# Issuing the sixteen block transfers of each head group from one queue instead of two

## Chip, core and metric

The kernel runs on one NeuronCore of a Trainium2 chip. The metric is the device time of one execution in microseconds (us); several runs are given by their median. The engines are named as the profile names them: PE (TensorE, matrix products), DVE (VectorE), ACT (ScalarE), POOL (GpSimd) and SP (SyncE). SP computes nothing here: it only issues transfers (DMAs). ACT computes and also issues some transfers. "SPq" and "ACTq" in the profile are the issuing of transfers by these two engines.

## What is computed

A decoder layer on `x` of 4 batches of 1024 tokens with 256 features: self-attention, cross-attention to 64 context tokens, and a routed feed-forward part, each on a layer norm of `x` and added to `x`. All is in float32. The part that matters here is the self-attention, with 16 query heads, 4 key/value heads and a head size of 64:

```python
qkv = hidden_states @ qkv_w.T + qkv_b
xq, xk, xv = jnp.split(qkv, [H * D, H * D + KV * D], axis=-1)
...
xq = xq * scale[None, None, None, :]
xk = jnp.repeat(xk, rep, axis=2)
xv = jnp.repeat(xv, rep, axis=2)
scores = jnp.einsum('bqhd,bkhd->bhqk', xq, xk)
probs = jax.nn.softmax(scores.astype(jnp.float32), axis=-1).astype(xq.dtype)
out = jnp.einsum('bhqk,bkhd->bqhd', probs, xv)
out = out.reshape(B, S, H * D)
return out @ o_w.T + o_b
```

## The kernel before

**The unit of work.** A "duo" (function `duo`, line 561 on) is the attention of 4 heads for one tile of 128 query tokens of one batch. There are 4 batches x 8 query tiles x 4 duos = 128 duos. For each of the 4 heads PE computes the scores of 128 queries against 1024 keys (line 587), DVE takes the maximum of each row (line 601), ACT writes the exponentials into the tile `prob` and sums them (line 607), and DVE transposes each 32x32 block in place (line 616). PE needs the weights with the keys on the partitions, so the blocks must also be exchanged between the four groups of 32 partitions. That is done by sixteen transfers from the tile `prob` to the tile `probT`, for each pair of a source group `qb` and a target group `r` (lines 638 to 653, function `carry`). Each moves 32 partitions x 1024 float32, 128 KB, within the on-chip memory. Then PE multiplies the transposed weights by the values (line 668, tile `av`), and ACT copies the result to `heads` (line 683). After four duos `project` (line 688) divides by the sums and applies the output projection; for that three more transfers go through SP (line 714 `rsD`, and line 704 twice, `rb`).

**Who issues the sixteen.** The loop over `k` and `qb` issues them in four rounds of four. Rounds 0, 1 and 2 go through SP's queue (12 transfers), round 3 through ACT's (4 transfers), where they stand among ACT's own instructions. Each engine works its instructions in order, so an instruction that waits holds up all that stand behind it.

**Buffers.** `prob` and `probT` of all duos share four places of 16 KB per partition (`prob=4` in the table of places). A duo takes one for `prob` before its first exponential and one for `probT` before its first transfer. By the planner's allotment the places go round: in 107 of the 127 duos after the first, `probT` takes the place that held `prob` of the duo ahead of it, so that its first transfer must wait until all sixteen transfers of the duo ahead have landed. In most of the others it takes the place of an earlier `probT` and waits for that one's `av`.

**The order of the work.** Nothing is issued directly. Each step is recorded as a task with an engine, an assumed cost in us, the tiles that it reads and writes, and a due time (`flow.add`). The planner (`Flow.order`) then plays the tasks through with these costs and fixes in which order each engine's instructions are issued, and which place each buffer gets. The chip runs these fixed orders and synchronizes by semaphores. The costs given to the sixteen transfers are 0.68 on SP and 0.45 on ACT, and a landing time of 2.3 (`lag`). In the trace the transfers share eight completion semaphores (100 to 105, 107 and 108) that are given out in turn; a transfer waits until the one that had its semaphore before it, eight transfers back, has landed.

Of the kernel before, what the change touches and what calls it, by code (L numbers as in the profile page):

```python
# [77 lines left out]
class Flow:  # L78
# [14 lines left out]
    def add(self, engine, cost, key, emit, reads=(), writes=(), lag=None, holds=(), lead=False, urgent=False):  # L93
        t = Task(engine, cost, emit, key, self.LAG.get(engine, 0.0) if lag is None else lag)
        t.lead, t.urgent = lead, urgent or lead
        for b in reads:
            t.need.update(b.writers)
        for b in writes:
            t.need.update(b.readers)
        t.need.discard(t)  # L100
        for b in reads:
            b.readers.append(t)
        for b in writes:
            b.writers.append(t)
        for b in dict.fromkeys(x.whole for x in (*reads, *writes, *holds)):
            if b.tag is None:
                continue
            if not b.uses:
                t.takes.append(b)
                b.first = t  # L110
                if b.tag not in self.shared:
                    self.lines.setdefault(b.tag, []).append(b)
            elif b.first is not t:
                t.need.add(b.first)
            b.uses.add(t)
            t.bufs.append(b)
        self.tasks.append(t)
        return t
# [71 lines left out]
def decoder(  # L190
# [21 lines left out]
    nc = tc.nc  # L212
# [238 lines left out]
    def by_array(d):  # L451

        return False
# [107 lines left out]
    def duo(b, d):  # L561
# [16 lines left out]
        for i in range(2):  # L578
# [17 lines left out]
            for z in range(2):  # L596
                k = z * QC + c
# [37 lines left out]
        if not by_array(d):  # L635


            for k in range(4):
                for qb in range(4):
                    r = (qb + k) % 4  # L640

                    engine, queue, cost = ("ACT", nc.scalar, 0.45) if k == 3 else ("SP", nc.sync, 0.68)

                    def carry(qb=qb, r=r, queue=queue):
                        queue.dma_start(  # L645
                            out=probT.t[32 * r : 32 * r + 32, S * qb : S * (qb + 1)],
                            in_=prob.t[32 * qb : 32 * qb + 32, S * r : S * (r + 1)],
                        )

                    add(  # L650
                        engine, cost, at, carry, [prob.part((z, i)) for z in range(2) for i in range(2)],
                        [probT.part((z, g)) for z in range(2) for g in range(2)], lag=2.3,
                    )
# [529 lines left out]
    for b in range(B):  # L1183
        at = float(b * steps_of)
        normed(b, lambda g: at - 18 + 2 * g if b else -50 + g)
        for w in range(NT // 2):
            if w == 0:
                keys(b, 0, at - 5)
            for c in range(0, QC, 2):
                queries(b, w, c, at + 2 * QC * w + c - 5)  # L1190
            if w == 0:
                keys(b, 1, at - 1)
                for g in range(NT // 2):
                    value_rows(b, g, at + g / 2)
                for g in range(NT // TF):
                    load_x(b, g, at + 2 + 4 * g * QC)
                context(b, at + 10)
            for d in range(QC * w, QC * w + QC):
                duo(b, d)
                if d % (QC // 2) == QC // 2 - 1:  # L1200
                    project(b, d // (QC // 2))
            t = 2 * w + 1
            cross_attention(b, t - TX + 1, at + QC * (t + 1) + 3)
            last = TX if (b, t // TF) == (B - 1, NT // TF - 1) else TF
            if t % last == last - 1:
                feed_forward(b, t - last + 1, last, at + QC * (t + 1) + 10)
# [93 lines left out]
```

## Time and profile before

| | us |
|---|---|
| median of 3 runs | 1967.02 |
| lowest and highest run | 1962.63 and 1979.3 |
| the profiled execution | 1969.67 |
| its span (first to last instruction) | 1968.0 |
| PE busy in the span | 1664.0 |
| DVE busy | 1535.9 |
| ACT busy | 929.0 |
| POOL busy | 556.0 |
| issues of `probT<-prob` by SP / by ACT | 1536 / 512 |

The profile shows one execution. "Busy" leaves out the issuing of transfers, so ACT's 929.0 us hold nothing of the 512 transfers that it issues. Idle time of an engine is put down to what ended it. The chain of work that ended last follows the execution backwards from its end, at each step to what released it; its shares tell which work the end time hung on. The granted clock of PE is 0.916 of full speed as a mean over the span.

### The profile page before, as it was taken

The page shows a single profiled execution, that of the slowest core. Times are in us where ns is not written, and L with a number is a line of the kernel's source. Part 1 is how long each engine was busy: PE and PEld are TensorE (multiplying, and loading weights), DVE is VectorE, ACT ScalarE, POOL GpSimd, SP SyncE. Part 2 cuts the span into 40 slices and gives each one's busy share as a digit, 9 for nine tenths or more (in the row PEclk, how much of TensorE's full clock was granted, in tenths as well). Part 3 has the DMA queues.
Part 4 walks back from the last instruction along what each step waited for, and adds up shares of the span by engine and source line. Part 5 has one row for each costly group of instructions (what it writes and reads, how often), then busy time and mean ns, then how long its engine had stood idle before and what let it go on. Part 6 is the DMA issues. An engine that isn't in the chain of part 4 may idle for free.

```text
span 1968.0 us, 27927 instructions
## 1 busy us (share of the span) xinstructions
PE 1664.0 (85%) x9156; PEld 936.4 (48%) x9156; DVE 1535.9 (78%) x2164; ACT 929.0 (47%) x1721; POOL 556.0 (28%) x872
## 2 busy tenths in 40 slices
PE   6898997889998798889989788888999888887632
PEld 4454554545555454444545444444555544453321
DVE  4887887888788787798778878887879978789432
ACT  3454554545455454544445445554545545453211
POOL 1001222252222522243031522215112251214352
PEclk8999999989999999889999899988999999898755
DMA  3777777577675777567677577656767577765500
GB/s 132 182 184 189 180 174 185 132 189 184 153 183 125 178 188 177 129 154 181 161 179 175 129 177 188 153 147 167 172 168 183 135 176 178 176 157 129 132 13 12
DMA packets 120032, 310.14 MB, mean 158 GB/s; under 512 B 36560, under 2 KB 47568, under 8 KB 119888
## 3 DMA queue, kind: packets, MB, share of 16 engines
q1 hardware_dynamic: 91504, 229.39, 48.4%
q10 hardware_dynamic: 25680, 69.52, 14.6%
q0 software_dynamic: 2704, 9.46, 1.6%
q8 instruction: 74, 1.21, 0.3%
q14 instruction: 70, 0.57, 0.1%
HBM read 35.32 MB, written 4.46 MB: 20 GB/s over the span
## 4 chain that ended last, share of the span: by engine, by line
PE 40%; DMA 19%; DVE 14%; SPq 12%; ACT 5%; issue 5%; POOL 3%; ACTq 2%; DVEq 0%; POOLq 0%
PE av L668 16%; DMA probT<-prob 16%; PE s L587 12%; SPq L645 11%; DVE nmax L601 6%; PE po L725 3%; ACT prob L607 3%; DVE prob L616 3%; ACTq L645 2%; DMA rb<-rsD 1%; PE pq L540 1%; PE pk L489 1%; PE pxt L895 1%; PE pxp L929 1%; PE pv L512 1%
## 5 line engine op out<-in xcount | busy, mean ns | idle before, releaser
L607 ACT ACTIVATE prob<-s,nmax 128x1024 f32<-128x1024 f32 x512 | 569.2, 1113 | 530.1 <-DVE nmax L601 444.4
L601 DVE TENSOR_REDUCE nmax<-s 128x1 f32<-128x1024 f32 x512 | 599.4, 1211 | 192.8 <-PE s L587 191.2
L616 DVE STREAM_TRANSPOSE prob<-prob 128x1024 f32<-128x1024 f32 x512 | 612.1, 1221 | 69.7 <-ACT prob L607 56.6
L668 PE MATMUL av<-probT,vn 128*64 128x256 f32 x4096 | 543.6, 420 | 110.3 <-DMA probT<-prob 50.8
L587 PE MATMUL s<-kT,qT 64*128 64x512 f32 x2048 | 583.8, 628 | 34.7 <-ACT prob L607 34.7
L668 PEld LDWEIGHTS av<-probT,vn 128*64 128x64 f32 x4096 | 321.1, 151 | 349.6 <-issue 183.4
L587 PEld LDWEIGHTS s<-kT,qT 64*128 64x128 f32 x2048 | 213.0, 190 | 271.1 <-issue 177.2
L707 POOL TENSOR_TENSOR heads<-heads,rb 128x256 f32<-128x256 f32 x128 | 91.4, 734 | 517.6 <-DMA rb<-rsD 353.1
L540 PE MATMUL pq<-ln_T,wq 128*128 128x256 f32 x512 | 127.0, 392 | 1.5 <-ACT heads L683 0.8
L725 PE MATMUL po<-wo,heads 128*128 128x256 f32 x512 | 125.5, 389 | 1.7 <-POOL heads L707 1.4
L683 ACT COPY heads<-av 128x256 f32<-128x256 f32 x128 | 47.2, 369 | 152.8 <-PE av L668 137.3
L725 PEld LDWEIGHTS po<-wo,heads 128*128 128x128 f32 x512 | 92.7, 190 | 40.4 <-issue 17.7
L540 PEld LDWEIGHTS pq<-ln_T,wq 128*128 128x128 f32 x512 | 94.2, 192 | 35.8 <-issue 11.1
L860 POOL TENSOR_TENSOR xsc<-xsc,xmx 128x1024 f32<-128x1024 f32 x32 | 60.9, 1904 | 162.6 <-DVE xmx L857 158.2
L607 ACT ACTIVATION_READ_ACCUMULATOR prob<-s,nmax 128x1 f32 x512 | 100.3, 196 | 0.0
L551 ACT ACTIVATE qT<-pq,bqs,qscale 128x256 f32<-128x256 f32 x128 | 66.7, 564 | 34.2 <-PE pq L540 21.9
L882 POOL TENSOR_TENSOR xsc<-xsc,xrs 128x1024 f32<-128x1024 f32 x32 | 60.8, 1901 | 56.5 <-DVE xrs L879 56.0
L895 PE MATMUL pxt<-ident,xsc 128*128 128x128 f32 x256 | 43.9, 302 | 36.0 <-POOL xsc L882 31.1
L422 ACT ACTIVATE ln_n<-x,ln_mv,ln_rs 128x256 f32<-128x256 f32 x64 | 36.5, 595 | 72.5 <-POOL ln_mv L417 63.9
L414 POOL TENSOR_SCALAR ln_rs<-ln_mv 128x1 f32<-128x1 f32 (+1 forms) x96 | 21.4, 223 | 168.7 <-DVE ln_mv L410 150.2
L1120 POOL DMA_INDIRECT par<-in_table,tile x32 | 32.4, 1012 | 128.8 <-DVE tile L1109 122.9
L436 PE MATMUL ln_pt<-ident,ln_n 128*128 128x128 f32 x192 | 35.3, 306 | 37.1 <-ACT ln_n L422 28.7
(163 smaller groups left out, 1385.5 us busy)
## 6 DMA issues: line engine op xcount, KB each, us to landing
probT<-prob SPq DMA_DIRECT2D x1536, 128.0 KB, 3.1
probT<-prob ACTq DMA_DIRECT2D x512, 128.0 KB, 3.7
rb<-rsD SPq DMA_DIRECT2D x64, 256.0 KB, 4.2
ln_n<-in_x SPq DMA_DIRECT2D x16, 256.0 KB, 3.1
x<-in_x SPq DMA_DIRECT2D x8, 512.0 KB, 4.1
out<-ln_n POOLq DMA_DIRECT2D x7, 512.0 KB, 4.9
wq<-in_w_qT ACTq DMA_DIRECT2D x1, 1024.0 KB, 8.2
wo<-in_w_oT SPq DMA_DIRECT2D x1, 1024.0 KB, 12.7
```

The lines of the kernel that those rows point to most:

```text
L540: mm(pq.t[:, 2 * P * k : 2 * P * (k + 1)], lhsT=wq[:, dc, (c + k) * P : (c + k + 1) * P], rhs=xTs[b].t[:, dc, 2 * P * w : 2 * P * (w + 1)] ...
L551: nc.scalar.activation(qTs[b, w, c + k].t, pq.t[:, 2 * P * k : 2 * P * (k + 1)], AF.Identity, bias=bqs[:, c + k : c + k + 1], scale=qscale,)
L587: mm(ps[z].t[:, 512 * g : 512 * (g + 1)], lhsT=q.t[r, (qt % 2) * P : (qt % 2 + 1) * P], rhs=kT.t[r, 512 * g : 512 * (g + 1)], start=True, ...
L601: nc.vector.tensor_reduce(nmax.t, ps[z].t, AX.X, ALU.max, negate=True)
L607: nc.scalar.activation(weights(prob.t, z, i), src, AF.Exp, bias=nmax.t, accum_out=ss.t[:, k : k + 1])
L616: nc.vector.transpose(t, t)
L645: queue.dma_start(out=probT.t[32 * r : 32 * r + 32, S * qb : S * (qb + 1)], in_=prob.t[32 * qb : 32 * qb + 32, S * r : S * (r + 1)],)
L668: mm(av.t[r, : 2 * P], lhsT=vns[b, kc // 2].t[:, kc % 2, j * HD : (j + 1) * HD], rhs=rhs, start=(kc == 0), stop=(kc == NT - 1),)
L707: nc.gpsimd.tensor_tensor(hT[e].t, hT[e].t, rb.t[:, 2 * e : 2 * e + 2, :], ALU.mult)
L725: mm(po.t[:, :D], lhsT=hT[c // 2].t[:, c % 2], rhs=wo[:, c, :], start=(c == 0), stop=(c == QC - 1))
L860: nc.gpsimd.tensor_tensor(sc.t, sc.t, mx.t.unsqueeze(2).to_broadcast([P, XH, SK]), ALU.subtract)
L895: flip(pt.t[:, j * P : (j + 1) * P], flat[:, c * P : (c + 1) * P], ident)
```

## The change

All sixteen transfers are issued from SP's queue. The assumed cost, which the planner uses, becomes 0.64 for each. The transfers themselves, their order in the loop, their tiles and their sizes stay the same.

```diff
             for k in range(4):
                 for qb in range(4):
                     r = (qb + k) % 4
 
-                    engine, queue, cost = ("ACT", nc.scalar, 0.45) if k == 3 else ("SP", nc.sync, 0.68)
+                    engine, queue, cost = ("SP", nc.sync, 0.64)
 
                     def carry(qb=qb, r=r, queue=queue):
                         queue.dma_start(
```

Since the planner decides all orders, the changed engines and costs also move other instructions. In both versions each query tile's three transfers `rsD` and `rb` stand between or within these groups on SP's queue. On PE, the first `av` product of a duo stands on average 1.89 duos of score products behind its own scores before the change and 1.91 after it; it stands exactly two duos behind in 84 of the 128 duos before and in 109 after, and one and a half behind in 33 before and in 17 after. `probT` takes the place of the `prob` of the duo ahead in 107 of 127 duos before and in 121 after.

## Prediction

> **What bounds the kernel now.** I read the busy times first, then the chain that ended last, then one stretch where it is simple, then SP's queue, and last the waits of PE and ACT.
>
> ```profile
> PE 1664.0 (85%) x9156; PEld 936.4 (48%) x9156; DVE 1535.9 (78%) x2164; ACT 929.0 (47%) x1721; POOL 556.0 (28%) x872
> ...
> PE 40%; DMA 19%; DVE 14%; SPq 12%; ACT 5%; issue 5%; POOL 3%; ACTq 2%; DVEq 0%; POOLq 0%
> ```
>
> PE is the busiest engine, yet only 40% of the chain is PE's. DMA and SPq together have 31%: for a good part of the time the end hangs on issuing and landing transfers. The chain from 60 to 1800 us (start and end left out), and then from 100 to 130 us:
>
> ```profile
> by line: DMA probT<-prob 17.5%; PE av L668 17.3%; PE s L587 12.9%; SPq L645 12.9%; DVE nmax L601 5.9%; issue 4.5%; PE po L725 3.3%; ACT prob L607 3.1%; DVE prob L616 2.4%; ACTq L645 2.0%; DMA rb<-rsD 1.6%; PE pq L540 1.3%; PE pxt L895 1.0%;
> ```
> ```profile
> by line: DMA probT<-prob 49.5%; SPq L645 46.4%; issue 4.1%; ACT prob L607 3.9%; ACTq L645 0.5%
> ```
>
> From 100 to 130 the block transfers alone are 95.9% of the chain, though PE is busy 29.08 of these 30 us: there both bind. SP's timeline shows how. The first row is one duo's burst on SP, the second its last eight transfers alone, the third the start of the next burst; the fourth is ACT's share of the first burst, from ACT's timeline.
>
> ```profile
> 146.31 9.48 SPq L645 DMA_DIRECT2D probT<-prob  x12
> ...
> 150.79 5.00 SPq L645 DMA_DIRECT2D probT<-prob  x8
> ...
> 157.79 0.51 SPq L645 DMA_DIRECT2D probT<-prob  x1
> ```
> ```profile
> 146.21 2.83 ACTq L645 DMA_DIRECT2D probT<-prob  x4
> ```
>
> The burst ends at 155.79 and the next begins 2.00 us later, when the last transfer has landed, because the next `probT` takes the place of this `prob`. So bursts are a serial chain: burst, landing, burst, here with a period of 157.79 - 146.31 = 11.48 us. Over the trace 82 of 127 bursts start so: 1.6 to 3.5 us behind the burst ahead (mean 2.2), over 0.5 us after their own transposes were done. In the burst SP and ACT issue together at first; the eight that SP issues alone come every (5.00 - 0.59) / 7 = 0.63 us, at 0.59 us each by the median in this view, whose last line is the landing:
>
> ```profile
> L645 SPq DMA_DIRECT2D probT<-prob x1536: 507/590/2257, 50.8 to 1850.7; - x192
> L645 ACTq DMA_DIRECT2D probT<-prob x512: 513/613/2090, 53.1 to 1839.2; - x171
> ...
> DMA to landing us min/median/max: 2.2/3.2/6.9
> ```
>
> Last, what SP, then PE and ACT (60 to 1800 us), wait for:
>
> ```profile
> SPq L645 <- DMA probT<-prob: 340.8, 289, 5.3
> ...
> SPq L645 <- PE av L668: 80.1, 15, 14.9
> ```
> ```profile
> PE av L668 <- DMA probT<-prob: 49.4, 23, 3.7
> PE s L587 <- ACT prob L607: 32.9, 26, 2.8
> ```
> ```profile
> ACT prob L607 <- DVE nmax L601: 421.8, 182, 8.5
> ...
> ACT prob L607 <- DMA probT<-prob: 49.9, 14, 6.6
> ```
>
> PE waits at `av` for transfers more than for anything else; ACT mostly waits for DVE, so it has time to spare.
>
> **The change, part by part.** The sum is made against the profiled execution: span 1968.0, with 1.67 us around it 1969.67. It lies 2.65 us above the median 1967.02.
>
> *Four more issues on SP in each burst.* Alone on SP, sixteen take 15 x 0.63 + 0.59 = 10.04 us, against 9.48 in the burst shown: +0.56. The 93 bursts that nothing else interrupts have a median of 9.47 and a mean of 9.73, so +0.57 or +0.31. I take 0.56, since the mean contains late semaphores. Below, a gain is possible: all bursts, with `rsD` and `rb` inside and ACT's part counted, last 10.39 on average, 0.35 more than 10.04. Above, at the mean pitch of today's bursts (10.39 / 12 = 0.87, transfers delaying each other) sixteen would take 13.9: +3.5. I take 0.63, because it is the row of transfers on SP alone.
>
> How many count: SPq and DMA of these transfers are 30.4% of 1740 us = 529 us of the chain. Where nothing else binds they are 95.9% of it, so this is worth 529 / 0.959 = 552 us of pure burst chain, or 552 / 11.48 = 48 periods. 48 x 0.56 = **+27 us**. Bounds: 23 duos in which PE visibly waits at `av` for a landing, x 0.31 = +7; all 82 chained bursts x 0.56 = +46.
>
> *The landing behind a burst* stays 2.0: it comes after issues that SP already makes alone today. The wait for the semaphore of eight transfers back goes: on one queue that one was issued 8 x 0.63 = 5.04 us earlier, and landings have a median of 3.2. Today's burst contains such a wait (149.84 to 150.79); its going is within the 10.04.
>
> *Four issues taken from ACT.* All 512 take 340 us of ACT's queue (mean 0.66), and waiting for semaphores ahead of them 46 us. Most of it covers nothing, since ACT has those 421.8 us of waiting for DVE. What stands behind it are exponentials: 54 of 512 start late behind such an issue or wait, by 82.4 us together. Exponential, maximum and transpose have 11.4% of the chain from 60 to 1800, 198 us; all of them last 512 x (1.21 + 1.31 + 1.22) = 1915 us, so about one in ten is on it: 0.10 x 82.4 = **-8 us**. Bounds: 0 and -82.
>
> *What else is on SP.* `rsD` and `rb` of 32 query tiles now can stand behind up to four more issues, 2.5 us each: 32 x 2.5 = 80 us at most. I take 0: they release `heads` on POOL, and PE waits only 1.7 us for those in all. The input loads have due times far ahead.
>
> *The new order.* The planner's assumed burst on SP was 12 x 0.68 = 8.2 us, is now 16 x 0.64 = 10.2, and the chip's would be 10.04: `av` is placed more evenly (exactly two duos behind in 109 of 128 instead of 84). But the serial tie between bursts also holds in 121 of 127 duos instead of 107. No row prices this. Bounds from both sides are the 49.4 us of waiting at `av`, all gone, or as much again. I take 0.
>
> Sum: +27 - 8 = +19, so 1969.67 + 19 = **1989**, 1.1% above the median. What is late next is SP itself: its burst and landing take 12.0 us of a duo instead of 11.5, where a duo lasts 14.2 on average.
>
> A rule of the Trainium skill speaks for less. In "DMA: Bandwidth & Descriptors", section "Issuing engines are not separate DMA queues", it says that issuing from several engines at once saves only the sequencer's issue time, which is usually small beside the transfer. The first half agrees with the rows, but here sixteen issues take 10.04 us beside a landing of 3.2; were the issue time negligible, the sum would be rival 2's.
>
> **Rivals.**
>
> 1. *Faster: ACT's relief decides.* The late exponentials hold up transposes, and so the next burst, and PE's score tiles (PE waits 32.9 us for exponentials). For it: ACT idles 49.9 us ahead of exponentials until a transfer lands, up to 6.6 at a time. Against it: in chained bursts the transposes are done early. If half of the 82.4 us counts and bursts stay as long as now, 1969.67 - 41 = 1929. It decides once SP's burst grows by less than 41 / 48 = 0.85 us and half of the lateness is on the path.
> 2. *Nothing: the longer burst is covered.* `av` starts 5.8 us after the last issue on average, 3.8 beyond a landing of 2.0. If those 0.56 us stay within that, and PE (97% busy from 100 to 130 us) is what binds: 1970. Against it: PE waits at `av` 23 times.
> 3. *Much slower: the transfers delay each other, not the queue.* With 13.9 us a burst, 48 x 3.5 = +168: 2138. For it: the 16 DMA engines are busy 0.81 from 100 to 130 us. Against it: SP alone keeps 0.63 over eight in a row.
>
> **How the numbers follow.** Forecast case 0.50, rival 1 0.27, rival 2 0.20, rival 3 0.03. The time is the first one's, 1989; with its bounds (+7 - 8, and +46 without relief, the new order at a quarter of its bounds on either side) it runs from 1957 to 2028. The range takes in rival 2 and the upper part of rival 1 and leaves out rival 3: 1940 to 2028. A measurement of this kernel can tell about 1% (20 us) from no change. Slower by over 1%: 0.41 of the forecast case and rival 3, 0.44. Faster: 0.25 of rival 1 and 0.02 of rival 2 by the new order, 0.27. Within 1%: the rest, 0.29.
>
> **What would show it.** Right: uninterrupted bursts of 16 on SP near 10.0 us, starts 2.0 us behind the burst ahead, SPq and DMA at more than 31% of the chain, the longer wait of `av` for transfers on PE. ACT's waits for `probT` transfers gone in any case. Wrong: bursts below 9.5 or above 11 us (pitch mis-taken), PE's wait at `av` falling below 49 us (the new order or ACT's relief decided), or the chain moving from SP to PE with an unchanged time (rival 2).

## The result, and the profile after

The changed kernel takes 1954.09 us (median of 11 runs, 1944.91 to 1959.58) against 1967.02 before: a ratio of 0.9932, 95% interval 0.991 to 0.9954, so 13 us faster. The forecast was 1989, slower by 1.1%. The sign was wrong.

The busy times and the chain by engine, from the page of the changed kernel (its span is 1949.9):

```profile
PE 1669.0 (86%) x9156; PEld 950.6 (49%) x9156; DVE 1556.7 (80%) x2164; ACT 931.0 (48%) x1721; POOL 556.8 (29%) x872
...
PE 45%; SPq 20%; DVE 14%; DMA 8%; ACT 5%; issue 5%; POOL 2%; DVEq 0%; POOLq 0%; ACTq 0%
```

PE is no less busy (1664.0 before); what fell is its idle time, from 1968.0 - 1664.0 = 304.0 to 280.9 us. ACTq is gone from the chain, and SPq and DMA together have 28% of it, where they had 31%. The chain from 60 to 1800 us, then from 100 to 130:

```profile
by line: SPq L645 19.7%; PE s L587 16.3%; PE av L668 15.4%; DMA probT<-prob 7.7%; DVE nmax L601 4.9%; issue 4.8%; PE po L725 3.8%; ACT prob L607 3.2%; DVE prob L616 2.9%; PE pq L540 2.2%; PE pk L489 1.3%; PE pxq L811 1.3%; PE pv L512 1.3%; 
```
```profile
by line: SPq L645 76.2%; DMA probT<-prob 23.4%; issue 5.7%
```

In the early stretch the chain still is nothing but transfers, with more issuing (46.4% before, 76.2% now) and less landing. From 60 to 1800 us the same: landings fall from 17.5 to 7.7%, issuing rises from 12.9 to 19.7%. An undisturbed burst, from SP's timeline, and all issues of the line:

```profile
166.21 10.02 SPq L645 DMA_DIRECT2D probT<-prob  x16
```
```profile
L645 SPq DMA_DIRECT2D probT<-prob x2048: 507/590/2216, 50.4 to 1847.6; - x187
...
DMA to landing us min/median/max: 2.2/2.4/6.4
```

What SP waits for, then PE and ACT from 60 to 1800 us:

```profile
SPq L645 <- DMA probT<-prob: 187.6, 219, 3.7
```
```profile
PE s L587 <- ACT prob L607: 50.0, 30, 6.1
PE av L668 <- DMA probT<-prob: 26.0, 16, 3.5
```
```profile
ACT prob L607 <- DVE nmax L601: 415.9, 187, 6.7
...
ACT prob L607 <- DMA probT<-prob: 65.0, 25, 4.7
```

SP's own waiting for transfers nearly halves (340.8 before). PE's waiting at `av` falls from 49.4 to 26.0, the opposite of what longer bursts should do, but its waiting for exponentials rises from 32.9 to 50.0. Between 60 and 1800 us the two nearly cancel, as the same 1740 us of both kernels show (columns: time, then busy time and number of instructions of PE, PEld, DVE, ACT and POOL, then clock, DMA share and GB/s; before first, after second):

```profile
60.00:1800.00 1740.00, 1547.03 (x8636) 867.02 (x8637) 1436.60 (x1897) 866.80 (x1611) 480.33 (x720) 0.94 0.70 167
60.00:1800.00 1740.00, 1550.19 (x8618) 879.79 (x8620) 1457.72 (x1916) 868.33 (x1611) 492.38 (x743) 0.94 0.72 167
```

PE's idle time here is 193.0 us before and 189.8 after, and the number of products is nearly the same. Of the 23.1 us by which its idle time falls, 20.6 lie behind 1800 us, where the last duos and the work after them run (93.5 before, 72.9 after).

The bursts are longer: over the trace, bursts that nothing interrupts have a mean of 10.62 (9.73 before) and a median of 10.43 (9.47), and 98 of 127 start chained (82).

Early in the program this costs what it should. The same columns for 168 us, before first, after second:

```profile
62.00:230.00 168.00, 153.32 (x845) 83.64 (x843) 140.53 (x144) 84.64 (x158) 25.57 (x32) 0.97 0.79 189
```
```profile
62.00:230.00 168.00, 147.92 (x775) 82.93 (x777) 126.13 (x125) 77.28 (x145) 18.57 (x24) 0.93 0.76 176
```

The changed kernel gets 775 products done where the old one got 845. Duo 16 (counted from 0) ends its `av` at 274.8 instead of 262.0: 13 us behind. Then it catches up slowly. As a mean over the 32 duos of a batch it is 10.4 us behind in the first, 6.3 in the second, 0.1 in the third, and 0.1 ahead in the fourth. Single duos scatter by 10 us and more around this. The last duo ends 13.3 us ahead.

### The profile page after: what moved, and what is told of

The parts are those of the page before. It is cut to its first block, busy times and chain, and to the rows that moved or that the text cites. A ratio compares the mean times of both kernels' runs of the same rounds, so it can differ in the third digit from the quotient of the medians.

```text
span 1949.9 us, 28055 instructions
## 1 busy us (share of the span) xinstructions
PE 1669.0 (86%) x9156; PEld 950.6 (49%) x9156; DVE 1556.7 (80%) x2164; ACT 931.0 (48%) x1721; POOL 556.8 (29%) x872
## 4 chain that ended last, share of the span: by engine, by line
PE 45%; SPq 20%; DVE 14%; DMA 8%; ACT 5%; issue 5%; POOL 2%; DVEq 0%; POOLq 0%; ACTq 0%
SPq L645 19%; PE s L587 15%; PE av L668 14%; DMA probT<-prob 7%; DVE nmax L601 5%; PE po L725 4%; DVE prob L616 3%; ACT prob L607 3%; PE pq L540 2%; PE pk L489 2%; PE pxq L811 1%; PE pxp L929 1%; PE pv L512 1%; PE pxt L895 1%; PE ln_pt L436 1%
## 5 line engine op out<-in xcount | busy, mean ns | idle before, releaser
L587 PE MATMUL s<-kT,qT 64*128 64x512 f32 x2048 | 601.5, 640 | 51.4 <-ACT prob L607 50.9
L668 PE MATMUL av<-probT,vn 128*64 128x256 f32 x4096 | 511.2, 403 | 79.9 <-DMA probT<-prob 29.5
L668 PEld LDWEIGHTS av<-probT,vn 128*64 128x64 f32 x4096 | 311.5, 145 | 289.8 <-issue 118.4
L587 PEld LDWEIGHTS s<-kT,qT 64*128 64x128 f32 x2048 | 219.8, 192 | 289.7 <-issue 176.5
L540 PE MATMUL pq<-ln_T,wq 128*128 128x256 f32 x512 | 137.0, 415 | 4.5 <-ACT qT L551 2.2
L860 POOL TENSOR_TENSOR xsc<-xsc,xmx 128x1024 f32<-128x1024 f32 x32 | 61.1, 1910 | 238.2 <-DVE xmx L857 209.2
L540 PEld LDWEIGHTS pq<-ln_T,wq 128*128 128x128 f32 x512 | 100.4, 205 | 51.2 <-issue 24.2
L551 ACT ACTIVATE qT<-pq,bqs,qscale 128x256 f32<-128x256 f32 x128 | 68.4, 564 | 35.6 <-PE pq L540 35.5
L935 POOL TENSOR_TENSOR x<-x,xres 128x256 f32<-128x256 f32 x32 | 23.2, 726 | 182.6 <-DVE xres L932 182.6
L731 POOL TENSOR_TENSOR x<-x,res 128x256 f32<-128x256 f32 x32 | 23.4, 730 | 166.1 <-DVE res L728 166.1
```

The lines of the kernel that those rows point to most:

```text
L540: mm(pq.t[:, 2 * P * k : 2 * P * (k + 1)], lhsT=wq[:, dc, (c + k) * P : (c + k + 1) * P], rhs=xTs[b].t[:, dc, 2 * P * w : 2 * P * (w + 1)] ...
L551: nc.scalar.activation(qTs[b, w, c + k].t, pq.t[:, 2 * P * k : 2 * P * (k + 1)], AF.Identity, bias=bqs[:, c + k : c + k + 1], scale=qscale,)
L587: mm(ps[z].t[:, 512 * g : 512 * (g + 1)], lhsT=q.t[r, (qt % 2) * P : (qt % 2 + 1) * P], rhs=kT.t[r, 512 * g : 512 * (g + 1)], start=True, ...
L668: mm(av.t[r, : 2 * P], lhsT=vns[b, kc // 2].t[:, kc % 2, j * HD : (j + 1) * HD], rhs=rhs, start=(kc == 0), stop=(kc == NT - 1),)
L860: nc.gpsimd.tensor_tensor(sc.t, sc.t, mx.t.unsqueeze(2).to_broadcast([P, XH, SK]), ALU.subtract)
```

## The experiments

The change does two things: it moves four issues, and it changes the planner's input and with that every engine's order. The first four runs take these apart. Theory A: freeing ACT brought more than the longer bursts cost. Theory B: the bursts cost what was forecast, and the new order brought the gain. Theory C: longer bursts are covered, and neither matters much. A ratio is always to the kernel before on the same chip; differences between runs are worked out from the ratios, times 1967 us.

**E1, the move alone.** The planner still believes in ACT at 0.45, so PE, DVE and POOL keep the order of before, and ACT too, but for the four issues.

```diff
-  engine, queue, cost = ("ACT", nc.scalar, 0.45) if k == 3 else ("SP", nc.sync, 0.68)
+  engine, queue, cost = ("ACT", nc.sync, 0.45) if k == 3 else ("SP", nc.sync, 0.68)
```

> The planner keeps the costs and engines of before, so PE, DVE and POOL have exactly the order of before; only the queue that issues round 3 becomes SP's. Theory A (ACT's relief is worth more than the 8 us I gave it): faster than before, 1945 to 1958. Theory B (the changed order brought the gain, the longer bursts cost what I forecast): 1980 to 1995. Theory C (a longer burst is covered nearly everywhere, and neither matters): 1962 to 1972.

Measured: 2022.58, ratio 1.0258 (1.0219 to 1.0296), 51 us slower. The chain and PE's waits from 60 to 1800 us:

```profile
by line: SPq L645 32.2%; PE av L668 12.9%; PE s L587 10.8%; DMA probT<-prob 9.8%; issue 5.3%; DVE nmax L601 4.8%; PE po L725 2.7%; DVE prob L616 2.3%; ACT prob L607 2.1%; SPq L704 1.2%; PE pq L540 1.2%; DMA rsD<-rsT 1.0%; PE pxp L929 1.0%; 
```
```profile
PE av L668 <- DMA probT<-prob: 73.5, 22, 5.3
```

This is what had been forecast, only larger: the chain moves to SPq, PE waits longer at `av`. Theory A falls for this order: with ACT freed and nothing else changed, the kernel is slower. Theory C falls too. In the early stretch E1 stands where the changed kernel does (`av` of duo 16 ends at 274.8 in both). It never catches up: by the means over the batches it is 2.4, 25.4, 41.8 and 57.8 us behind the changed kernel.

**E2, the order alone.** The changed plan, but ACT issues round 3.

```diff
-  engine, queue, cost = ("SP", nc.sync, 0.64)
+  engine, queue, cost = ("SP", nc.scalar if k == 3 else nc.sync, 0.64)
```

> The reverse: the order of the changed kernel on PE, DVE and POOL, planned with sixteen transfers on SP at 0.64, but ACT issues round 3 as before. Theory A (ACT's relief): no faster than before, 1965 to 1990, since ACT has its 512 issues back. Theory B (the order): 1920 to 1945, the gain without the longer bursts. Theory C: as the changed kernel, about 1954.

Measured: 2037.32, ratio 1.0329 (1.0295 to 1.0363). No theory had that. What SP waits for in E2:

```profile
SPq L645 <- DMA probT<-prob: 636.4, 409, 7.1
```

ACT's transfers now stand in its queue where the plan had meant SP to issue them. SP, which shares the eight semaphores, waits 636.4 us, where it waited 340.8 in the kernel before; of these, 426 us (160 before) end with the landing of a transfer that ACT issued. The uninterrupted bursts of twelve on SP last 10.63 us in the mean, as long as the sixteen of the changed kernel. So the gain is not a better order as such: this order is good for one queue only. Read the other way round, from E2 to the changed kernel, the same move of four issues saves 1.0329 - 0.9932 = 0.0397, 78 us.

**E3, another order for one queue**, planned at 0.68 per transfer instead of 0.64.

```diff
-  engine, queue, cost = ("SP", nc.sync, 0.64)
+  engine, queue, cost = ("SP", nc.sync, 0.68)
```

> All sixteen transfers on SP, but planned at 0.68 each instead of 0.64: the physical change is the same, the order differs from both. It shows how much the order alone moves the time. Theory A: 1945 to 1965, near the changed kernel. Theory B: anything from 1940 to 1990; over 10 us away from 1954 speaks for it.

Measured: 1984.63, ratio 1.0067 (1.0042 to 1.0092): 27 us from the changed kernel by the order alone, with the same transfers on the same queue.

**E4, a seventeenth transfer** in each burst, in the changed kernel's order. It copies 2 KB that nothing reads.

```diff
+                        if (k, qb) == (1, 0):
+                            queue.dma_start(out=dump, in_=prob.t[32 * qb : 32 * qb + 32, S * r : S * r + 16])
```

> The changed kernel with a seventeenth transfer in each burst, of 32 rows x 64 bytes into a scratch tile, in the same order: one more issue, hardly any data. It measures what 0.63 us more of a burst cost. If bursts are on the path as I counted (48 periods): 1954 + 30 = 1984. If every burst counted: 1954 + 81 = 2035. If the burst is covered: 1954 to 1958. Theory A alone says nothing on it; theory C wants the last.

Measured: 2004.04, ratio 1.0158 (1.0124 to 1.0191) against 0.9932 for the changed kernel: 0.0226 x 1967 = 44 us more. Its issue lasts as long as that of 128 KB, and uninterrupted bursts grow to a mean of 11.27:

```profile
L651 SPq DMA_DIRECT2D dump<-prob x128: 507/591/1897, 54.3 to 1891.2; - x128
```

128 x 0.65 = 83 us were added to bursts, 44 came out: about 0.53 of each burst's growth is on the path, 68 bursts' worth. I had counted 48, for the kernel before.

**E5 and E6: is an order a draw, or does it follow the planned cost?** One queue with six other planned costs, then the split kernel with two. The edits, for 0.60 each:

```diff
-  engine, queue, cost = ("SP", nc.sync, 0.64)
+  engine, queue, cost = ("SP", nc.sync, 0.60)
```
```diff
-  engine, queue, cost = ("ACT", nc.scalar, 0.45) if k == 3 else ("SP", nc.sync, 0.68)
+  engine, queue, cost = ("ACT", nc.scalar, 0.45) if k == 3 else ("SP", nc.sync, 0.60)
```

> All sixteen on SP, planned at 0.60 each; the chip's own pace in the changed kernel is 0.63. Theory F (the order is good because it was planned with the pace that the chip has): slower than 1954, as the plan puts the value products too early, 1960 to 1990, and PE's wait at av for transfers is above the 26 us of the changed kernel. Theory N (an order is a draw, and 0.64 happened to draw a good one): anywhere from 1940 to 1990, with no relation to the distance from 0.63.

> As the last, planned at 0.62. Theory F: 1950 to 1962, next to the changed kernel, since it is as near to the chip's pace. Theory N: anywhere from 1940 to 1990.

> Planned at 0.66, half way to the 0.68 that gave 1985. Theory F: 1958 to 1978, between the two. Theory N: anywhere from 1940 to 1990.

> Planned at 0.72. Theory F: slower than at 0.68, 1990 to 2030, with PE's wait at av for transfers at or below 12 us, because the value products stand too late. Theory N: anywhere from 1940 to 1990.

> All sixteen on SP, planned at 0.57. Theory G (a planned burst somewhat shorter than the real one gives the best order; far too short, PE waits at av, as with the order of before): near the best, 1935 to 1955. If the trend from 0.72 to 0.60 simply goes on: about 1932. Theory N (chance): anywhere from 1930 to 1990.

> Planned at 0.54, a burst of 8.6 us, near the 8.2 us that the order of before assumes and that gave 2023 with all sixteen on SP. Theory G: past the best, 1950 to 1990, with PE's wait at av for transfers above 40 us. If the trend goes on: below 1935.

> The kernel before (twelve on SP, four on ACT), with SP's transfers planned at 0.60 instead of 0.68: a planned burst of 7.2 us, where the chip's lasts 10.4 on average. Theory G: slower than before, 1975 to 2010. If shorter is better here too: below 1960.

> The kernel before with SP's transfers planned at 0.76: a burst of 9.1 us, nearer to the chip's 10.4. It asks whether the gain came from the queue or only from a better order, which two queues could have as well. If only from the order: 1935 to 1957. If one queue has an advantage of its own (ACT free): 1960 to 1985.

**E7: the split kernel's own best, and the bottom for one queue**, by the same two edits.

> The kernel before, SP's transfers planned at 0.72, between 0.68 (1970) and 0.76 (1942). A smooth curve: 1948 to 1964. Chance: anywhere from 1935 to 1990.

> The kernel before, planned at 0.80, a burst of 9.6 us, where the chip's was 10.4. If the best planned burst is a little shorter than the real one, as with one queue (9.6 against 10.6): the best of the split, 1925 to 1945; below 1930 it beats every order with one queue. Chance: anywhere from 1935 to 1990.

> The kernel before, planned at 0.84, a burst of 10.1 us. Past the best if one queue is the model (0.64 to 0.66 there): 1940 to 1965. Chance: anywhere from 1935 to 1990.

> All sixteen on SP, planned at 0.59, between 0.57 (1955) and 0.60 (1940). A smooth curve: 1938 to 1955. Chance: anywhere from 1930 to 1990.

Measured, with PE's wait at `av` for these transfers from 60 to 1800 us, and PE's busy and idle time over the span:

| one queue, planned cost | us | ratio (interval) | wait at `av` | PE busy | PE idle |
|---|---|---|---|---|---|
| 0.54 | 1984.82 | 1.0078 (1.0052 to 1.0104) | 68.4 | 1670.1 | 310.1 |
| 0.57 | 1954.71 | 0.9929 (0.9903 to 0.9954) | 36.7 | 1669.8 | 284.2 |
| 0.59 | 1943.35 | 0.9879 (0.985 to 0.9909) | 41.8 | 1650.5 | 286.1 |
| 0.60 | 1940.29 | 0.9851 (0.9818 to 0.9883) | 34.8 | 1656.8 | 285.4 |
| 0.62 | 1951.72 | 0.9919 (0.9889 to 0.995) | 32.9 | 1655.9 | 290.0 |
| 0.64, the changed kernel | 1954.09 | 0.9932 (0.991 to 0.9954) | 26.0 | 1669.0 | 280.9 |
| 0.66 | 1960.21 | 0.9955 (0.9929 to 0.9982) | 16.3 | 1691.6 | 270.4 |
| 0.68 | 1984.63 | 1.0067 (1.0042 to 1.0092) | 11.6 | 1692.5 | 288.2 |
| 0.72 | 2015.94 | 1.025 (1.0215 to 1.0285) | 14.3 | 1701.4 | 309.2 |

| two queues, planned cost on SP | us | ratio (interval) | wait at `av` | PE busy | PE idle |
|---|---|---|---|---|---|
| 0.60 | 1970.53 | 1.0006 (0.9982 to 1.0029) | 49.4 | 1659.4 | 310.5 |
| 0.68, the kernel before | 1967.02 | 1 | 49.4 | 1664.0 | 304.0 |
| 0.72 | 1911.90 | 0.9712 (0.968 to 0.9744) | 27.8 | 1641.6 | 266.9 |
| 0.76 | 1941.83 | 0.9856 (0.9806 to 0.9906) | 11.8 | 1671.4 | 270.8 |
| 0.80 | 1956.10 | 0.9941 (0.9915 to 0.9968) | 13.6 | 1665.0 | 287.7 |
| 0.84 | 1945.70 | 0.9886 (0.986 to 0.9912) | 11.5 | 1674.9 | 267.5 |

For one queue it is a valley, not a draw: theory N falls there. But its bottom is at 0.60, below the chip's pace of 0.63, so theory F falls as well; theory G had it right for one queue.

The two walls are of different kinds. On the left `av` stands too early in PE's order, and PE waits for transfers: from 0.60 to 0.54 its idle time grows by 25 us and its wait at `av` by 34, while the wait for exponentials shrinks. First 0.60, then 0.54:

```profile
PE s L587 <- ACT prob L607: 59.9, 34, 5.6
PE av L668 <- DMA probT<-prob: 34.8, 16, 3.4
```
```profile
PE av L668 <- DMA probT<-prob: 68.4, 28, 5.3
PE s L587 <- ACT prob L607: 41.0, 28, 6.8
```

On the right waits are the smaller part. From 0.60 to 0.72 the span grows by 68 us: PE's idle time by 24, its busy time by 45, for the same products. 0.66 even has the least idle time of all and is 20 us slower than 0.60. Busy times at 0.60, then at 0.72, then the waits at 0.72:

```profile
PE 1656.8 (85%) x9156; PEld 945.3 (49%) x9156; DVE 1544.4 (80%) x2164; ACT 933.4 (48%) x1721; POOL 556.7 (29%) x872
```
```profile
PE 1701.4 (85%) x9156; PEld 959.8 (48%) x9156; DVE 1554.2 (77%) x2164; ACT 935.9 (47%) x1721; POOL 558.7 (28%) x872
```
```profile
PE s L587 <- ACT prob L607: 69.2, 33, 6.1
...
PE av L668 <- DMA probT<-prob: 14.3, 7, 3.3
```

The granted clock goes with it: 0.917 at 0.60, 0.906 at 0.66, 0.912 at 0.68 and 0.900 at 0.72. By an estimate from these, 1656.8 x 0.917 / 0.900 - 1656.8 = 31 of the 45 us are the clock. Why a later order is granted less clock these runs do not show.

For two queues the curve is not smooth: 0.72 gives 1912, 57 us below 0.68 and 28 below 0.76, 0.80 is slower than both its neighbours, and 0.60 is not slower than 0.68, which theory G had expected it to be. So the expectations for 0.72 and 0.80 missed, and a good part of a single order's time is a draw there. The 0.72 order beats both kernels, and every order with one queue that was tried.

**E8, the move alone, in two more orders.** As E1, with SP's planned cost 0.72 and 0.76:

```diff
-  engine, queue, cost = ("ACT", nc.scalar, 0.45) if k == 3 else ("SP", nc.sync, 0.72)
+  engine, queue, cost = ("ACT", nc.sync, 0.45) if k == 3 else ("SP", nc.sync, 0.72)
```

> The order of the split kernel planned at 0.72 (1912), with all sixteen transfers on SP. Theory B (the move itself costs, whatever the order): 1912 + 30 to 65 = 1942 to 1977. If E1's price was a misfit of one order: 1905 to 1925.

> The same for the split order planned at 0.76 (1942). Theory B: 1972 to 2007. If E1's price was a misfit of one order: 1935 to 1955.

Measured: 1972.05, ratio 1.0024 (1.0003 to 1.0045), where the split kernel with that order had 0.9712: 61 us slower by the move. And 1965.49, ratio 0.9984 (0.9949 to 1.0019), against 0.9856: 25 us slower. PE's wait at `av` rises from 27.8 to 61.1 and from 11.8 to 30.2, as it rose from 49.4 to 73.5 in E1. The 0.72 order with all on SP:

```profile
PE av L668 <- DMA probT<-prob: 61.1, 29, 5.1
```

So the move costs 25 to 61 us in the three orders that were planned for two queues (0.76 missed the 1972 to 2007 of theory B by 6.5 us), and saves 78 us in the one planned for one queue (E2). In these runs the price goes with SP's burst. The mean of uninterrupted bursts grows by 0.69 us in the 0.76 order (25 us dearer), 0.84 in E1 (51), 1.08 in the 0.72 order (61), and not at all from E2 to the changed kernel. All three orders in which the move costs were planned with four transfers on ACT. How much of the price is that misfit, and how much the longer burst would cost in any order, is not separated. E4, which adds 0.65 us to the bursts of an order planned for one queue, costs 44 us.

## Why the prediction was wrong

**The step that failed is "The new order. ... No row prices this. ... I take 0."** Between E1 and the changed kernel the queues are the same and only the order differs. It is worth 1.0258 - 0.9932 = 0.0326, 64 us, more than all other terms, and beyond the 49.4 us that I gave as its bound. PE's idle time is 342.6 us in E1 and 280.9 in the changed kernel, 61.7 less, of which 47.5 is the wait at `av` for transfers (73.5 to 26.0); the wait for exponentials grows by 17 (33.1 to 50.0). The prediction's own sign for this came true: PE's wait at `av` fell below 49 us.

Its hint at the direction (`av` placed more evenly) is not shown to be the reason. By the same count as in "The change", the order of 0.72 with one queue has 126 of 128 duos exactly two behind and is the slowest, while the two-queue order of 0.72 has 97 and is the fastest.

A second step failed with it: the move and the order were priced apart and added. The move alone costs 51 us, the order alone (E2) 65, and the two together gain 13. Neither has a price of its own.

**Four more issues on SP (+27):** the mechanism held, the size did not. The shortest undisturbed bursts are 10.0 us (forecast 10.04), the start behind the burst ahead still 2.0 us by the median, the issues 0.59. Inside uninterrupted bursts SP's waits for transfers all but vanish, as forecast: 2.5 us in all, 102.6 before. But only 32 of 87 such bursts stay below 10.1 us, because in others single issues last over 0.8 us. So the median grew by 0.96 and the mean by 0.89, not by 0.56. How many bursts count was too low as well: by E4 68 of 128 bursts' growth comes through, not 48. The net of this and ACT's relief was put at +19; in the order of before it measures 51, in two others 61 and 25.

**ACT's relief (-8):** no run isolates it. In E1 exponentials start 201 us in all behind the end of their maximum, instead of 235: 34 us less, not 82. In the changed kernel it is 121 us, so the new order takes off more of this than the move. "ACT's waits for `probT` transfers gone in any case" was wrong: exponentials wait 65.0 us for such transfers, more than the 49.9 before. They are not ACT's own transfers, since ACT issues none now, but those that must land before a place for `prob` is free.

**The landing behind a burst, and `rsD` and `rb`:** as forecast. The starts keep 2.0 us, and PE's idle time at `po` is 1.9 us (1.7 before). The lower end of the forecast case, 1957, should by its own terms be 1956; nothing hangs on it.

**The rivals.** 1954 lies inside the stated range only by the part that was there for rival 1, and that is luck: rival 1 had the sign, not the cause. E1 shows that in the order of before ACT's relief does not pay for the longer bursts. In the changed order it cannot be told from the fit of the order, since E2, which gives ACT its issues back, also holds up SP. Rival 2 is refuted by E1 and E4, rival 3 by the bursts. The rule of the Trainium skill ("DMA: Bandwidth & Descriptors", "Issuing engines are not separate DMA queues") says that issuing from several engines saves only issue time, usually small beside the transfer. The first half agrees with E1: with all on SP the bursts last 0.84 us longer, while landings get no longer (2.3 us by the median). The "usually small" does not hold for these bursts: one issue takes 0.59 us beside a landing of 2.4, sixteen take 10.02, and the issuing is 20% of the chain.

**What stays open.** Why one order is better than another with the same queues is shown only as far as the two walls of the valley: the wait at `av` on the left, more busy time at a lower clock on the right. Why these orders differ so was not isolated, nor which of the moved instructions makes 1912 at 0.72 out of 1967 at 0.68; and since the split kernel's curve jumps, neither is 1912 known to be its best. That the change as a whole came out as a gain rests on the cost of 0.64 that was planned: planned at 0.68, the same move loses 0.7%.

## What to carry to other kernels

When a change to a queue also changes a planner's costs, two changes are made: run the physical one with the old order, and the old queues with the new order, before crediting either. Here the move costs 25 to 61 us in orders planned for two queues, the order planned for one queue costs 65 on two, and together they gain 13. A moved term should not be priced at zero because no row shows it; re-planning alone moved this kernel by up to 76 us (1940 to 2016). And look at busy time beside waits: a part of what an order costs can lie in the clock.

## What was not expected of the hardware

An issue of 2 KB and one of 128 KB take the same on SP's queue: 591 and 590 ns by the median. Issued from one queue, the 128 KB transfers land after 2.4 us instead of 3.1 on SP and 3.7 on ACT in the kernel before. It is not the second queue as such: in E2, where both issue too but SP mostly waits while ACT does, they land after 2.5 us on both. In the kernel before, transfers whose issue overlaps one of the other queue have a median landing of 3.9 us on either.
